# Gates projected a half block ahead, ranks and token transposes a step later: one reordering of a gated linear attention and mixture-of-experts kernel

## The chip, the cores and the metric

The kernel runs on one core of one Trainium2 chip. A core has TensorE (PE in the profile; its weight loads are PEld), VectorE (DVE), ScalarE (ACT), GpSimd (POOL) and SyncE (SP), which here only issues transfers. Each engine works through its own queue in order and waits on semaphores of the others. The metric is the device time of one execution in microseconds (us), the median of several runs.

## What is computed

The input x is 4 sequences of 2048 tokens with 256 features. The result is x plus two branches, both of the layer-normalised x:

```python
x = L0_attn_x
xn = _layernorm(x, axis=-1)
x = x + _L0_attn_ref(xn, ...) + _L0_ffn_ref(xn, ...)
```

The attention branch is a gated linear attention with 8 heads, keys of 128 and values of 64 features:

```python
q = (x @ Wq).reshape(B, S, H, DK)
k = (x @ Wk).reshape(B, S, H, DK) * DK ** (-0.5)
v = (x @ Wv).reshape(B, S, H, DV)
alpha = jax.nn.sigmoid((x @ Wg + bg) / GATE_NORM)
def step(state, inp):
    qt, kt, vt, at = inp
    state = at[..., None, None] * state + kt[..., None] * vt[:, :, None, :]
    return (state, jnp.einsum('bhk,bhkv->bhv', qt, state))
...
og = jax.nn.sigmoid(x @ Wog)
return out * og @ Wo
```

The other branch routes each token to 8 of 64 experts, which lie in 8 groups. The score of a group is the sum of its two best experts, the best 4 groups stay, and the 8 best experts within them are taken. An expert takes at most 256 tokens, in token order.

```python
group_scores = jax.lax.top_k(sfc.reshape(n, G, E // G), 2)[0].sum(-1)
gidx = jax.lax.top_k(group_scores, TG)[1]
...
topk_idx = jax.lax.top_k(tmp, K)[1]
pos = jnp.take_along_axis(jnp.cumsum(oh, 0) - 1, e[:, None], 1)[:, 0]
valid = pos < CAP
y = jnp.einsum('eci,eih->ech', jax.nn.silu(g) * u, w_down)
```

## The kernel before

**Two streams of work.** The attention goes through 32 blocks of 256 tokens (`block(s)`), each of two chunks (`ck`) of 128 tokens and two halves of 4 heads (`half`). A *unit* (s, half, ck) is one chunk of one half. The recurrence is done chunk by chunk: within a chunk by a masked product of scores, between chunks by a state of 128 x 64 per head. Beside it runs the routing, in batches of 512 tokens: `front(b)` normalises tokens, transposes them and makes the logits, `decays(i)` makes the decay factors of a group of batches, `back(b)` picks groups and experts and counts. All 16 batches are routed during the first 16 blocks. From block 16 on, the side stream is the experts.

**Steps.** `front`, `decays` and `back` are generators. `block` calls `step()` 12 times, and each call moves every generator that is due by one `yield`. Batch b's `back` starts at step 12 b + 3 (step 12 b + 1 is the first of block b), `front(b)` for b over 2 at step 12 (b - 2), and `decays` at a step set in the list near the end. When block 16 begins, the list of generators must be empty; then the memory of the routing is given to the experts.

**Order on the queues.** The order of the calls is a program order. A scheduler then makes each engine's queue from it by a model of time of its own, so that the order of a queue follows the program only roughly. `tc.issue_after(x)` keeps what is issued within it behind x.

**A half block**, on TensorE: state products of the two units done before (`dp`), decay differences (`lp`), keys of two groups of heads (`wk`), scores (`sp`), queries (`wq`), transposes of the keys (`kp`), the output projection of the chunk before (`wo`), values of the next block (`wv`), scores, gate (`wog`), and at the end the outputs (`od`) of two units. Each projection is three matmuls (high part by high part, high by low, low by high) in 16-bit parts. A projection of two heads or of one half of the gate is 12 matmuls of 128 x 256.

**The names that matter below.** In `project` the tile `pj` comes from the pool `ps["pj"]` with 4 buffers in this stage; a buffer is free when its readers are done. `split` (lines 220 and 221) reads it twice: ScalarE writes the high part (`k`, `qh`), then VectorE the low part (`k`, `ql`). VectorE also makes `qt` (line 860). `unit_a` makes the scores `sp` (one buffer), `unit_m` multiplies them on VectorE by the decay factors `dc` (line 929). `outputs` (lines 945 and 951) needs that product, the state and, on VectorE, the gate: `oT` is `od` times `og` plus 1 (line 959). `states` makes `dp` and, on VectorE, the new state (lines 979 and 982). `gate` makes one half of the heads' gate `og` with Tanh on ScalarE (line 827). `turn_tokens` transposes 512 tokens (`tp`, line 330) after ScalarE (line 390) and GpSimd (line 391) have made their two parts `x16`, and VectorE copies them out (line 331).

In `back`, lines 511 to 514 compare the group scores with one another: VectorE makes `cg` and `ce`, GpSimd masks and adds them. Then VectorE reduces `rank` (line 516), makes `gm` and `pen` (518, 520), GpSimd makes `tmp` (522, 523), VectorE takes maxima (530), replaces them (533) and makes `sel` (536). TensorE counts (`cp`, 541), VectorE makes `cr` (552), which SyncE stores to `cnt_d` (555). The first thing the experts do is read these counts back (line 594) and take differences on VectorE (`dd`, line 597).

**The start.** Before block 0, queries, keys, values and both gates of block 0 are made (`gate(0, 0)`, `gate(0, 1)`), then the first unit: scores, transposed keys, product and outputs. The units of which outputs and states are due stand in the list `done`.

Of the kernel before, what the change touches and what calls it, by code (L numbers as in the profile page):

```python
# [62 lines left out]
def bc(ap, axis, n):  # L63

    a = ap.unsqueeze(axis)
    shape = list(a.shape)
    shape[axis] = n
    return a.to_broadcast(shape)
# [3 lines left out]
def gla_moe_kernel(ctx: ExitStack, tc: tile.TileContext, x, Wq, Wk, Wv, Wo, Wg, bg, Wog,  # L72
# [70 lines left out]
    made = {}  # L143
# [180 lines left out]
    def turn_tokens(x16, xT):  # L324
        for t in range(0, RT, 2):
            tp = ps["mo"].tile([P, 2, 2, 2, P], F16, tag="mo", name="tp")
            for t2 in range(2):
                for a in range(2):
                    for c in range(2):
                        nc.tensor.transpose(tp[:, t2, a, c, :], x16[:, t + t2, a, c * P:(c + 1) * P], identh)  # L330
            nc.vector.tensor_copy(xT[:, t:t + 2], tp)

    def front(b):
# [61 lines left out]
                                       in_=flat.bitcast(F32)).ins  # L395
        yield True
        if b >= 2:
            turn_tokens(x16, xT)
            yield True
        stored = nc.sync.dma_start(out=xT_d[b], in_=xT)  # L400
# [78 lines left out]
    def back(b):  # L479
# [32 lines left out]
        nc.vector.tensor_tensor(ce, ga, gb, ALU.is_equal)  # L512
        nc.gpsimd.tensor_tensor(ce, ce, bc(tri, 1, RT), ALU.mult)
        nc.gpsimd.tensor_tensor(cg, cg, ce, ALU.add)
        rank = r1.tile([P, RT * G], F32, name="rank")
        nc.vector.tensor_reduce(rank, cg.rearrange("p t a b -> p (t a) b"), AX.X, ALU.add)
        gm = r1.tile([P, RT * G], F32, name="gm")
# [195 lines left out]
    def expert_late():  # L713

        for eng, lo, full, hi in moe["late"]:
            eng.tensor_tensor(lo, full, hi, ALU.subtract)  # L716
        moe["late"] = []

    def expert_step(new):

        q = list(moe["at"])
        if not new:

            q = [it for it in q if it[2] == len(expert_stages) - 1]
        if new and moe["next"] < E:
            e = moe["next"]
            moe["at"].append([e, fetch(e), 0])
            moe["next"] += 1
            look(e + AHEAD + 1)
        mids = []  # L730
        for it in q:
            e, m, st = it
            if st == len(expert_stages):
                continue
            expert_stages[st](e, m)
            if st == 2:
                mids.append((e, m))
            it[2] += 1
        for e, m in mids:
            expert_split(e, m)  # L740
        moe["at"] = [it for it in moe["at"] if it[2] < len(expert_stages)]


    side = []
# [4 lines left out]
    def step():  # L749

        now = clock[0]
        clock[0] += 1
        with ExitStack() as es:
            if len(anchor) > 1:
                es.enter_context(tc.issue_after(anchor[-2]))
            for it in list(side):
                if it[0] <= now and next(it[1], None) is None:
                    side.remove(it)
        if "at" in moe:
            owed[0] += EXPERTS / STEPS  # L760
            new = owed[0] >= 1.0
            if new:
                owed[0] -= 1.0
            expert_late()
            if new or moe["next"] >= E:
                expert_step(new)
# [52 lines left out]
    def two_heads(t, i):  # L819
        return t[:, :, 2 * i:2 * i + 2, :].rearrange("p c h t -> p c (h t)")  # L820

    def gate(s, i):

        if i == 0:
            blk[s]["og"] = ogp.tile([P, NCK, 4, P], F32, name="og")
        pj = project(s, "wog", i * 2 * P, P)
        nc.scalar.activation(two_heads(blk[s]["og"], i), pj, AF.Tanh, scale=og_fit)
# [66 lines left out]
    def unit_l(s, half, ck):  # L894

        B = blk[s]
        h0 = half * 4
        lp = ps["pj"].tile([P, 4, P], F32, tag="pj", name="lp")
        nc.tensor.matmul(lp.rearrange("p h i -> p (h i)"), lhsT=B["aj"][:, ck, :],  # L899
                         rhs=B["mv"][ck][:, h0:h0 + 4, :].rearrange("p h i -> p (h i)"),  # L900
                         start=True, stop=True)
        dc = dcp.tile([P, 4, P], F32, name="dc")
        nc.scalar.activation(dc, lp, AF.Relu, scale=-1.0)
        nc.scalar.activation(dc, dc, AF.Exp, scale=-1.0)

        if "at" in moe:
            nc.vector.tensor_tensor(dc, dc, bc(u_le, 1, 4), ALU.mult)
        else:
            nc.gpsimd.affine_select(out=dc, in_=dc, pattern=[[0, 4], [1, P]], compare_op=ALU.is_ge,
                                    fill=0.0, base=0, channel_multiplier=-1)  # L910
        B["dc", half, ck] = dc
# [14 lines left out]
    def unit_m(s, half, ck):  # L926
        B = blk[s]
        dc = B["dc", half, ck]
        anchor.append(nc.vector.tensor_tensor(dc, B["sp"], dc, ALU.mult).ins)  # L929
# [33 lines left out]
    def states(units):  # L963

        units = [u for u in units if (u[0] * NCK + u[2] + 1) % (SEQ // P)]
        if not units:
            return
        dp = ps["pj"].tile([P, 2, 4, DV], F32, tag="pj", name="dp")
        for n, (s, half, ck) in enumerate(units):
            kt, vw = blk[s]["kt"][half][:, ck * 8:ck * 8 + 8], blk[s]["vw"][ck]  # L970
            with tc.issue_after(made["od"]):
                for i in range(4):
                    product(dp[:, n, i, :], (kt[:, i, :], kt[:, 4 + i, :]),
                            tuple(t[:, half * 4 + i, :] for t in vw))
        for n, (s, half, ck) in enumerate(units):
            B = blk[s]
            new = w2.tile([P, 4, DV], F32, tag=f"state{half}", name=f"state{half}")
            if (s * NCK + ck) % (SEQ // P) == 0:
                nc.vector.tensor_copy(new, dp[:, n])
            else:  # L980
                B["aux"].tensor_tensor(new, state[half], bc(B["wall"][half][:, ck, :], 2, DV), ALU.mult)
                nc.vector.tensor_tensor(new, new, dp[:, n], ALU.add)
            state[half] = new
# [45 lines left out]
    done = []  # L1029

    def block(s):

        n = s + 1 < NS
        states(done)
        if s:
            split_o(s - 1, 1)
        if n:  # L1040
            load_block(s + 1)
            load_el(s + 1, 0)
        unit_l(s, 0, 1)
        keys(s, 1, 0)
        step()
        unit_a(s, 0, 1)
        keys(s, 1, 1)
        unit_l(s, 1, 0)
        step()
        unit_m(s, 0, 1)  # L1050
        queries(s, 1, 0)
        step()
        queries(s, 1, 1)
        turn_keys(s, 1, 0)
        if s:
            output(s - 1, 1)
        step()
        if s:
            finish(s - 1)
        if n:  # L1060
            values(s + 1, 0)
        unit_a(s, 1, 0)
        turn_keys(s, 1, 1)
        if s:
            gate(s, 1)
        step()
        unit_m(s, 1, 0)
        done[:] = (s, 0, 1), (s, 1, 0)
        outputs(done)
        step()  # L1070

        states(done)
        split_o(s, 0)
        if not n:
            unit_l(s, 1, 1)
            unit_a(s, 1, 1)
            output(s, 0)
            unit_m(s, 1, 1)
            outputs([(s, 1, 1)])
            split_o(s, 1)  # L1080
            step()
            return
        load_el(s + 1, 1)
        unit_l(s, 1, 1)
        keys(s + 1, 0, 0)
        step()
        unit_a(s, 1, 1)
        keys(s + 1, 0, 1)
        unit_l(s + 1, 0, 0)
        step()  # L1090
        unit_m(s, 1, 1)
        queries(s + 1, 0, 0)
        step()
        queries(s + 1, 0, 1)
        turn_keys(s + 1, 0, 0)
        output(s, 0)
        step()
        values(s + 1, 1)
        unit_a(s + 1, 0, 0)
        turn_keys(s + 1, 0, 1)  # L1100
        gate(s + 1, 0)
        step()
        unit_m(s + 1, 0, 0)
        done[:] = (s, 1, 1), (s + 1, 0, 0)
        outputs(done)
        step()
# [90 lines left out]
    def start_front(b):  # L1197
        return 0 if b < 2 else 6 if b == 2 else (b - 2) * STEPS

    for b in range(NB):  # L1200
        if b:
            f = front(b)
            side.append((start_front(b), f))
            if b == 1:
                with after(made["lt2"]):
                    next(f)
        side.append((b * STEPS + (3 if b else 0), back(b)))
        for i, (b0, nb_) in enumerate(DGROUPS):
            if i and b0 + nb_ - 1 == b:
                side.append((start_front(b) + (11 if b > 2 else 6), decays(i)))  # L1210

    unit_l(0, 0, 0)
    unit_a(0, 0, 0)
# [2 lines left out]
    step()  # L1216
    unit_m(0, 0, 0)
    done.append((0, 0, 0))
    outputs(done)
    for s in range(NS):  # L1220
        if not side and "at" not in moe:
            for _ in lists():
# [43 lines left out]
```

## Time and profile before

| | |
|---|---|
| median of 3 runs | 1251.77 us (1251.25 to 1252.61) |
| the profiled execution | 1252.01 us, its span 1250.0 us |
| blocks 2 to 15 (with routing), each | 34.3 us on the mean |
| blocks 17 to 29 (with experts), each | 41 to 44 us |
| TensorE's granted clock over the span | 0.995 of full |
| transfers over the span | 139 GB/s |

The span is the time from the first to the last instruction that the profile shows. The length of a block is the distance between the VectorE products of line 929, of which every block has four. In rows of the profile, a line gives start, duration, engine, source line, operation, what is written and read, and in brackets the idle time of the engine just before and what ended it. TensorE's matmuls overlap in the pipeline: one of 128 x 256 lasts 0.27 us in its row, and the next starts 0.11 us after it. So the distance from start to start, not the duration, is what a matmul costs when TensorE is full. Tables of stretches give the busy time of each engine in a stretch; the column after the five engines is the granted clock of TensorE.

### The profile page before, as it was taken

The numbers are of one execution on the slowest core, as the hardware profiler recorded it, in microseconds if no ns is written. First come the engines' busy times: TensorE is split into PE (matmuls) and PEld (weight loads), VectorE is DVE, ScalarE is ACT, GpSimd is POOL, SyncE is SP. The second block draws the span as 40 slices with busy tenths as digits, with TensorE's granted clock in tenths as the row PEclk, the third lists the DMA queues.
The fourth block names the chain that finished last, engine by engine and source line by source line (L and its number), as shares of the span: only waits on it lengthen the run. The fifth ranks groups of instructions, "written<-read, shape, count | busy, mean of one in ns | idle before, by whom it ended". The sixth has DMA issues, their size and how long they took to land.

```text
span 1250.0 us, 34808 instructions
## 1 busy us (share of the span) xinstructions
PE 1191.4 (95%) x13783; PEld 1040.7 (83%) x13783; DVE 973.5 (78%) x2669; ACT 857.5 (69%) x1536; POOL 709.3 (57%) x899
## 2 busy tenths in 40 slices
PE   6799999989999999999899999999999999999997
PEld 6587888877888878878789989999988898998986
DVE  6987778786787877777878878787878788887674
ACT  4567666666667567654667777777777777778764
POOL 1476667765666566653426656637757567565330
PEclk9899999999999999999999999999999999999999
DMA  7434444434334443323637676767767678666531
GB/s 244 158 123 127 131 122 117 126 87 114 97 112 127 135 127 110 108 52 78 181 87 152 163 160 137 169 151 178 157 156 167 148 167 180 150 138 150 111 60 35
DMA packets 148579, 165.35 MB, mean 132 GB/s; under 512 B 32384, under 2 KB 119296, under 8 KB 147712
## 3 DMA queue, kind: packets, MB, share of 16 engines
q1 hardware_dynamic: 114896, 113.57, 29.6%
q0 software_dynamic: 29712, 45.89, 21.5%
q10 hardware_dynamic: 3808, 3.67, 0.8%
q8 instruction: 108, 1.77, 0.6%
q14 instruction: 55, 0.45, 0.1%
HBM read 115.98 MB, written 58.38 MB: 139 GB/s over the span
## 4 chain that ended last, share of the span: by engine, by line
PE 68%; DVE 13%; POOL 6%; ACT 5%; DMA 5%; issue 3%; SPq 1%; DVEq 0%; POOLq 0%; ACTq 0%
PE pj L269 11%; PE pj L271 11%; PE pj L270 11%; PE od L945 4%; PE kp L884 3%; PE od L951 3%; DMA el<-el_d 3%; PE gu L269 2%; PE gu L271 2%; PE gu L270 2%; PE xet L646 2%; PE sp L270 2%; PE sp L269 2%; PE sp L271 2%; PE lp L899 1%
## 5 line engine op out<-in xcount | busy, mean ns | idle before, releaser
L702 POOL DMA_INDIRECT out_dram<-y,idx x128 | 211.6, 1653 | 93.1 <-issue 25.4
L626 POOL DMA_INDIRECT xe<-xw_d,idx x128 | 133.5, 1043 | 127.2 <-ACT y L688 86.9
L269 PE MATMUL pj<-xs,wq_h 128*128 128x256 f16 x496 | 135.4, 273 | 6.6 <-DVE k L221 4.6
L269 PE MATMUL pj<-xs,wk_h 128*128 128x256 f16 x496 | 135.6, 273 | 0.0
L271 PE MATMUL pj<-xs,wk_l 128*128 128x256 f16 x496 | 135.5, 273 | 0.0
L270 PE MATMUL pj<-xs,wk_h 128*128 128x256 f16 x496 | 135.5, 273 | 0.0
L270 PE MATMUL pj<-xs,wq_h 128*128 128x256 f16 x496 | 135.2, 273 | 0.0
L271 PE MATMUL pj<-xs,wq_l 128*128 128x256 f16 x496 | 135.2, 273 | 0.0
L929 DVE TENSOR_TENSOR dc<-sp,dc 128x512 f32<-128x512 f32 x128 | 87.7, 685 | 45.8 <-PE sp L271 28.4
L221 DVE SCALAR_TENSOR_TENSOR k<-pj,k 128x512 f16<-128x512 f32 x128 | 87.1, 683 | 40.1 <-ACT k L220 40.1
L220 ACT ACTIVATE k<-pj 128x512 f16<-128x512 f32 x128 | 75.2, 591 | 55.4 <-PE pj L271 55.1
L945 PE MATMUL od<-dc,v 128*64 128x128 f32 x1024 | 101.5, 280 | 7.3 <-DVE dc L929 7.3
L270 PE MATMUL sp<-ql,k 128*128 128x128 f16 x512 | 96.1, 220 | 5.5 <-DVE ql L221 5.2
L269 PE MATMUL sp<-qh,k 128*128 128x128 f16 x512 | 98.2, 220 | 0.0
L271 PE MATMUL sp<-qh,k 128*128 128x128 f16 x512 | 96.1, 220 | 0.0
L220 ACT ACTIVATE qh<-pj 128x512 f16<-128x512 f32 x128 | 76.0, 597 | 27.0 <-PE pj L271 26.8
L951 PE MATMUL od<-qt,state 128*64 128x128 f32 x960 | 94.4, 273 | 0.0
L989 ACT CAST oh<-oT 128x512 fp32r<-128x512 f32 x64 | 39.6, 618 | 79.5 <-DVE oT L959 79.5
L221 DVE SCALAR_TENSOR_TENSOR ql<-pj,qh 128x512 f16<-128x512 f32 x128 | 86.8, 679 | 9.2 <-ACT qh L220 9.1
L716 DVE TENSOR_TENSOR wl<-w,wh 128x768 fp32r<-128x768 f32 x64 | 61.2, 956 | 40.9 <-ACT wh L650 39.3
L884 PE MATMUL kp<-identh,k 128*128 128x128 f16 x1024 | 83.0, 220 | 8.7 <-DVE k L221 5.4
L860 DVE SCALAR_TENSOR_TENSOR qt<-pj,el 128x512 f32<-128x512 f32 x128 | 86.7, 678 | 0.0
(408 smaller groups left out, 4533.6 us busy)
## 6 DMA issues: line engine op xcount, KB each, us to landing
el<-el_d SPq DMA_DIRECT2D x64, 512.0 KB
xw_d<-x SPq DMA_DIRECT2D x16, 512.0 KB
xT_d<-xT SPq DMA_DIRECT2D x16, 512.0 KB
out_dram<-in_L_attn_x_dram SPq DMA_DIRECT2D x16, 512.0 KB
w<-in_L_ffn_w_gate_dram SPq DMA_DIRECT2D x64, 128.0 KB
w<-in_L_ffn_w_up_dram SPq DMA_DIRECT2D x64, 128.0 KB
w<-in_L_ffn_w_down_dram SPq DMA_DIRECT2D x64, 128.0 KB
xs<-xT_d SPq DMA_DIRECT2D x31, 256.0 KB
```

The costliest lines, as they stand in the source:

```text
L220: return (nc.scalar.activation(hi, t, AF.Copy, scale=scale).ins, nc.vector.scalar_tensor_tensor(lo, in0=t, scalar=scale, in1=hi, op0=ALU.m ...
L221: nc.vector.scalar_tensor_tensor(lo, in0=t, scalar=scale, in1=hi, op0=ALU.mult, op1=ALU.subtract).ins)
L269: nc.tensor.matmul(out_, lhsT=a[0], rhs=b[0], start=first, stop=False)
L270: nc.tensor.matmul(out_, lhsT=a[0], rhs=b[1], start=False, stop=False)
L271: return nc.tensor.matmul(out_, lhsT=a[1], rhs=b[0], start=False, stop=last).ins
L626: in_turn(lambda: nc.gpsimd.indirect_dma_start(out=xe[:, f, :], out_offset=None, in_=xw_d[:, :], in_offset=bass.IndirectOffsetOnAxis(ap=id ...
L702: two = [in_turn(lambda: nc.gpsimd.indirect_dma_start(out=of, out_offset=bass.IndirectOffsetOnAxis(ap=idx[:, e, f:f + 1], axis=0), in_=m[" ...
L860: read = nc.vector.scalar_tensor_tensor(qt, in0=pj, scalar=QFIT, in1=two_heads(el, i), op0=ALU.mult, op1=ALU.mult)
L884: nc.tensor.transpose(kp[:, i, :], k[:, i, :], identh)
L929: anchor.append(nc.vector.tensor_tensor(dc, B["sp"], dc, ALU.mult).ins)
L945: mm = nc.tensor.matmul(od[i * DV:(i + 1) * DV, n, j, :], lhsT=v[:, h0 + 2 * j + i, :], rhs=dc[:, 2 * j + i, :], start=True, stop=first)
L951: mm = nc.tensor.matmul(od[i * DV:(i + 1) * DV, n, j, :], lhsT=state[half][:, 2 * j + i, :], rhs=qt[:, ck, 2 * j + i, :], start=False, sto ...
```

## The change

Five edits in the order of calls; no computation is added or left out.

- The outputs of the first unit move from the end of the start into block 0, behind two more groups of keys.
- As no outputs have been made by then, the first `states` has nothing to stand behind, and does without.
- The gates of block s + 1 are made in the two halves of block s: the first half in the first, the second in the second. Before, the gate of the first half was made in the second half of block s, and that of the second half in the first half of block s + 1.
- `back` yields once more ahead of `rank`, so that `rank` and all behind it come a step later. It then ends in the twelfth step of its block and not in the eleventh.
- `front` of batches 3 and on yields once more ahead of `turn_tokens`, and `decays` of these starts a step later.

```diff
@@ front
         if b >= 2:
+            if b > 2:
+                yield True
             turn_tokens(x16, xT)
             yield True
@@ back
         nc.gpsimd.tensor_tensor(cg, cg, ce, ALU.add)
+        yield True
         rank = r1.tile([P, RT * G], F32, name="rank")
@@ states
-            with tc.issue_after(made["od"]):
+            with tc.issue_after(made["od"]) if "od" in made else ExitStack():
@@ block, first half
         keys(s, 1, 1)
         unit_l(s, 1, 0)
+        if s == 0:
+            outputs(done)
         step()
...
         turn_keys(s, 1, 1)
-        if s:
-            gate(s, 1)
+        if n:
+            gate(s + 1, 0)
         step()
@@ block, second half
         turn_keys(s + 1, 0, 1)
-        gate(s + 1, 0)
+        gate(s + 1, 1)
         step()
@@ the list of generators
-                side.append((start_front(b) + (11 if b > 2 else 6), decays(i)))
+                side.append((start_front(b) + (12 if b > 2 else 6), decays(i)))
@@ the start
     done.append((0, 0, 0))
-    outputs(done)
     for s in range(NS):
```

`n` is true in all blocks but the last.

## The prediction

> **What bounds the kernel now.** I read the page's first part, then the engines' busy time by stretch, then TensorE's waits, and last the single stalls in order of time.
>
> ```profile
> PE 1191.4 (95%) x13783; PEld 1040.7 (83%) x13783; DVE 973.5 (78%) x2669; ACT 857.5 (69%) x1536; POOL 709.3 (57%) x899
> ```
>
> TensorE is busy for 1191.4 of 1250.0 us, so 58.6 us of idle TensorE is all that reordering can win. The stretches show where it lies (columns: us, length, then busy time of PE, PEld, DVE, ACT and POOL with instruction counts, granted clock, DMA share, GB/s):
>
> ```profile
> 66.00:580.00 514.00, 488.68 (x5901) 414.44 (x5902) 404.50 (x1199) 336.79 (x606) 331.28 (x587) 1.00 0.38 111
> 580.00:650.00 70.00, 65.22 (x741) 55.77 (x739) 52.45 (x147) 42.81 (x75) 24.40 (x24) 1.00 0.51 132
> 650.00:1180.00 530.00, 528.67 (x6003) 477.13 (x6001) 422.81 (x1072) 403.81 (x730) 317.74 (x236) 1.00 0.69 156
> 1180.00:1250.00 70.00, 63.21 (x730) 54.65 (x728) 41.10 (x80) 38.07 (x66) 15.07 (x10) 0.99 0.27 50
> ```
>
> From 650 to 1180 us (attention with experts) TensorE idles 1.3 us: nothing to win. From 66 to 580 us (attention with routing, blocks 1 to 15) it idles 25.3 us, in the hand-over to the experts 4.8 us, in the last stretch 6.8 us, and the rest, 20 us, before 66 us. The waits by cause:
>
> ```profile
> PE od L945 <- DVE dc L929: 7.3, 5, 2.9
> PE kp L884 <- DVE k L221: 5.4, 4, 1.8
> PE sp L270 <- DVE ql L221: 5.2, 8, 1.7
> PE pj L269 <- DVE k L221: 4.6, 7, 0.9
> PE tp L330 <- ACT x L390: 4.6, 3, 2.2
> ```
>
> **The change part by part.** TensorE, VectorE, ScalarE, GpSimd and SyncE get the same instructions, each as often as before (22450 on TensorE with its weight loads, 39 activation-table loads on ScalarE among them). Only places in the queues move, so the sum is made of stalls.
>
> *(a) The first unit's outputs follow the keys.* Stalls of TensorE that bear on this and the next parts (start, length, what waits, idle time before it and its releaser):
>
> ```profile
> 50.05 1.12 PE L945 MATMUL od<-dc,v 128*64 128x128 f32 x8 [2.91 <-DVE dc L929]
> 65.91 0.88 PE L945 MATMUL od<-dc,v 128*64 128x128 f32 x12 [2.27 <-DVE dc L929]
> 231.27 0.29 PE L330 MATMUL tp<-identh,x 128*128 128x128 f16 x2 [2.14 <-ACT x L390]
> 373.52 0.22 PE L270 MATMUL sp<-ql,k 128*128 128x128 f16 x1 [0.62 <-DVE ql L221]
> 441.03 0.28 PE L330 MATMUL tp<-identh,x 128*128 128x128 f16 x2 [2.18 <-ACT x L390]
> ```
>
> At 47.14 us TensorE stands before the first outputs until VectorE has made dc. Now the state products and the keys go first, and the 2.91 us look won. They are not, because VectorE is full here: from 50 to 66 us its rows follow each other with hardly a gap. In the new order of VectorE the product dc of the third unit (65.18 us now) has before it the same work, plus one copy of transposed keys (0.33 us from its start to the next start): about 65.5 us. So TensorE, which waits for that product at 65.91 us, gets there no earlier, and the stall only spreads: the lower key halves (55.90 and 59.93 us now) come at about 58.1 and 58.8 us by adding up the rows ahead of them in the new order, and TensorE's queries wait for the first of them. What can be won is the clock:
>
> ```profile
> 49.00:50.00 1.00, 0.00 (x0) 0.00 (x0) 0.69 (x2) 0.00 (x0) 0.57 (x3) 1.00 0.02 6
> 51.00:52.00 1.00, 1.00 (x15) 0.77 (x14) 0.86 (x6) 0.00 (x0) 0.01 (x1) 0.50 0.00 0
> 68.00:69.00 1.00, 1.00 (x20) 0.93 (x18) 1.00 (x3) 0.00 (x0) 1.00 (x2) 0.50 0.00 0
> ```
>
> After each of the two idle stretches the granted clock is 0.5 for some 3.4 us (0.55, 0.50, 0.50, 0.75 from 50 to 54 us; 0.58, 0.50, 0.50, 0.71 from 67 to 71 us), a loss of 1.7 us each. The first lies under VectorE's bound; the second does not, since TensorE has no wait from 66 to 96 us. With the idle time spread over more places I give the second back half the time: **-0.9 us**. Ends: -8.6 (2.91 + 2.27 + 2 x 1.7), were VectorE not the bound; +1.6, were all that the lower key halves come later to reach the end.
> The Trainium skill (TensorE: Matmul & The Clock Gate, "HAM oscillation") states that only idle gaps over about 3.4 us cost the clock. By that rule gaps of 2.91 and 2.27 us cost nothing and this term is 0; the trace shows half clock after both, and full clock after the 2.14 us at 231 us, so the rows decide.
>
> *(b) Gates half a block ahead.* A gate group is 12 matmuls of 0.11 us, start to start: 1.3 us. Every half block keeps one; block 0's first half gains one, the last block's loses one. In block 0 it falls into the idle 63.6 to 65.9 us and is free. In the last block the gate runs from 1234.43 to 1235.73 us and the outputs start at 1235.95 us; their factor dc is there at 1234.88 us. Without the gate they start at about 1235.0 us, as dc then ends the wait: **-0.9 us**. The cover that is gone is thus counted. Its activation (0.69 us of ScalarE) moves along; VectorE's oT has no wait for og in the trace. Ends: -1.3, 0.
>
> *(c) Token transposes a step later* (blocks from batch 3 on, 13 batches). At 231 and 441 us they wait 2.14 and 2.18 us for ScalarE's casts, at 96.68 us 0.30 us: 4.6 us. A step is 34.3 us / 12 = 2.86 us (dc rows at 94.15 and 574.42 us lie 14 blocks apart), more than each wait, so the casts are done. With them go the store of xT, the copy of x to the output, the gate logits, the table load for the sigmoid and the decays, all a step later on SyncE and ScalarE; the tokens are read by projections blocks later, so nothing waits. I keep 1.0 us for a new wait of the same size as the smaller ones in the list (0.2 to 0.9 us): **-3.6 us**. Ends: -4.6, +1.
>
> *(d) Ranks a step later.* In a half block of today (VectorE rows of one place):
>
> ```profile
> 371.02 0.61 DVE L530 MAX8 m<-tmp 128x8 f32<-128x64 f32 x4 [0.46 <-POOL tmp L523]
> 372.44 0.43 DVE L536 TENSOR_TENSOR sel<-tmp,rep 128x256 bf16<-128x256 f32 x1
> 372.78 0.68 DVE L221 SCALAR_TENSOR_TENSOR ql<-pj,qh 128x512 f16<-128x512 f32 x1
> 373.38 0.68 DVE L860 SCALAR_TENSOR_TENSOR qt<-pj,el 128x512 f32<-128x512 f32 x1
> ```
>
> ScalarE has qh at 372.17 us, yet ql starts at 372.78 us, behind the maxima, replacements and sel; TensorE's sp waits 0.62 us. In the new order keys, ql and qt mostly stand ahead of maxima and sel, and keys ahead of rank. In blocks 1 to 15 the waits for ql are 2.5 us in all (0.62, 0.18, 0.62, 0.62, 0.50) and for qt 0.9 us. I take 70% of 3.4: **-2.4 us**. The waits of projections for k (0.5 to 0.9 us each) I leave: there k waits for ScalarE behind a 1.28 us table load, and rank, gm and pen ahead of it run meanwhile. Ends: -7.0 (those 3.6 us and a further 1.0 too), +5 (second rival, its smaller form).
>
> *(e) Hand-over to the experts.* The counts of the last batch are also a step late: VectorE's cr stands just ahead of oT (585.36 us now) and not at 581.30 us, so some 3.5 us later, and the store (4.64 us) and reload (2.42 us) of the counts follow it. VectorE's first dd waits 3.25 us for them now and would wait about 4.2 us, the second 1.3 instead of 2.64 us, since keys and state now go ahead of the first. **0**. Ends: -1.5, and +2.9, the whole step.
>
> Sum: -0.9 - 0.9 - 3.6 - 2.4 + 0 = -7.8 us; the span goes from 1250.0 to 1242.2 us. The profiled execution took 1252.01 us, 2.0 us around its span, and the median is 1251.77: 0.24 less. So 1242.2 + 2.0 - 0.2 = **1244 us**.
>
> **The rivals.**
> *The whole VectorE side clears.* All waits for ql, qt and k at kp (3.6 us) go, 2.1 us of dc waits, the tp waits and most of the start: 4.6 + 3.4 + 3.6 + 2.1 + 0.9 + 6.9 = 21.5, or 1230 us. For it: VectorE is only 78% busy. Against: k is late behind ScalarE.
> *Ranks overfill a quarter (slower).* Between the products of the units (s,1,1) and (s+1,0,0) VectorE now has rank 0.42, gm and pen 1.27, maxima and replacements 1.28, sel 0.33, two xT 1.2, k 0.6, two ql and qt 2.4, kt 0.33, dc 0.6: 8.4 of the 8.6 us of a quarter block. Waits inside (0.3 for k, 0.6 for sp, 0.5 for POOL's cg) make an overrun of 1.2 us. TensorE's cover from sp to od is a gate and eight transposes, 1.3 + 0.44, of which dc takes 0.69: 1.06 us. Cost per batch is the overrun above that. At 1.2 us it takes 13 x 0.14 = 2 us; from 1.64 us on it eats the 7.8; at 2.2 us (gm at its longest, 0.92, and one more wait of POOL) it costs 14.8 and gives 1259 us. Against: sel, cr and xT may slip past dc in the queue, and in part do.
> *Only gate and tp pay*, as ql finds other work ahead of it: -4.5, and 1247.3 us.
> *The waits only move* and the change does nothing: 1251.8 us. For it: ScalarE's table loads and its wait for oT (2.96 us at 192 us) stay where they were.
>
> **How the numbers follow.** Forecast 0.42 (its own range 1239 to 1248), all of VectorE's side 0.15, gate and tp only 0.20, nothing 0.08, overfilled quarter 0.15. A measurement of this kernel tells about 0.2%, 2.5 us, from no change. Faster: 0.42 + 0.15 + 0.20 = 0.77; same 0.08; slower 0.15. The range, 1232 to 1255 us, leaves out some six tenths of each outer case (0.09 + 0.09, under 2 in 10).
>
> **What would show it.** (a) No 2.91 us stall at 47 us, dc of the third unit still near 65 us, granted clock near 1.00 from 67 to 71 us. (b) Outputs of the last block within 0.3 us of dc. (c) No tp wait over 1 us. (d) sp waits for ql under 1.5 us from 66 us on. (e) TensorE idle 4 to 6 us from 580 to 650 us. Wrong if TensorE idles as long as now from 66 to 580 us, or od waits for dc in most blocks.

## The result and the profile after

The changed kernel takes 1248.22 us (median of 10 runs, 1245.44 to 1249.80), the kernel before beside it 1252.45 us (10 runs, 1251.25 to 1254.33). The ratio is 0.9955, 95% interval 0.9943 to 0.9967: faster by 0.45%, which would be 5.6 us; the two medians lie 4.2 us (0.34%) apart, which the interval holds too. The profiled execution took 1247.5 us, its span 1245.6 us against 1250.0, so 4.4 us are to be found in the traces.

The engines' totals in the profile after: the counts of instructions are the old ones and TensorE is as busy as before, so the gain is idle time.

```profile
PE 1191.6 (96%) x13783; PEld 1039.2 (83%) x13783; DVE 967.7 (78%) x2669; ACT 858.6 (69%) x1536; POOL 710.5 (57%) x899
```

The stretches of the profile after (columns as in the prediction's table):

```profile
66.00:580.00 514.00, 490.73 (x5900) 415.45 (x5899) 397.12 (x1194) 336.75 (x605) 331.35 (x585) 0.99 0.38 112
580.00:650.00 70.00, 67.21 (x767) 58.14 (x764) 56.40 (x161) 45.65 (x78) 24.90 (x25) 1.00 0.52 140
```

TensorE's idle time from 66 to 580 us, where most of the gain was expected, went from 25.3 to 23.3 us only. From 580 to 650 us, where none was expected, it went from 4.8 to 2.8 us. Fixed windows cut the kernels at different places of the work, so the rest of this document measures stages by the VectorE products `dc` (line 929 before, 932 after; the new lines shift the later ones by up to 3). Each stage is the distance between the same two products in both kernels; in us, after less before:

| stage | after - before |
|---|---|
| first instruction to the first product (49.31 us before) | -0.5 |
| first product to the end of block 0 | +1.8 |
| end of block 0 to block 14 | -3.3 |
| block 14 to block 15 | +1.5 |
| hand-over: block 15 to block 16 | -2.9 |
| block 16 to block 30 | 0.0 |
| last block, to the last instruction | -1.0 |

They add up to the 4.4 us. Up to the end of block 15 the net is -0.4 us. A single stage ahead of block 17 is less sure than its sum: with every mark taken one product later, the stages from the first product on read -0.1, +0.8, -3.8 and +0.3 in place of +1.8, -3.3, +1.5 and -2.9. From block 17 to block 30 the distance to the old trace is the same to 0.1 us: TensorE is full there, and what was won ahead of it is carried to the end unchanged.

TensorE's waits by cause (us, times, longest), here from 66 to 580 us alone and not over the whole span as in the prediction, after:

```profile
PE pj L269 <- DVE k L221: 7.2, 8, 1.3
PE od L948 <- DVE dc L932: 6.3, 5, 2.5
PE tp L330 <- ACT x L390: 1.9, 2, 1.6
```

Against the same window before, the two waits that the change was costed on did fall: `tp` from 4.6 to 1.9 us, `sp` for `ql` from 2.5 to 1.5 us; `kp` for `k` from 3.6 to 0.9 us. But the projections' wait for `k` rose from 3.6 to 7.2 us and that of the outputs for `dc` from 4.4 to 6.3 us.

**Where the 2.1 us of `tp` went.** ScalarE's rows around 228 us in the kernel before (start, length, line, operation; in brackets its idle time and what ended it):

```profile
225.21 0.62 ACT L989 CAST oh<-oT 128x512 fp32r<-128x512 f32 x1 [2.99 <-DVE oT L959]
...
230.61 0.60 ACT L390 CAST x<-xt 128x512 f16<-128x512 f32 x1
```

The same place after:

```profile
228.68 0.62 ACT L992 CAST oh<-oT 128x512 fp32r<-128x512 f32 x1 [2.62 <-DVE oT L962]
...
231.65 1.07 ACT L220 ACTIVATE k<-pj 128x512 f16<-128x512 f32 x2
```

and the stall of TensorE that belongs to it:

```profile
233.00 0.27 PE L269 MATMUL pj<-xs,wq_h 128*128 128x256 f16 x1 [1.11 <-DVE k L221]
```

In both kernels ScalarE stands nearly 3 us before a cast that waits for `oT`; behind it stand decay factors with a table load of 1.28 us (226.34 and 229.82 us) and, before, four pieces of the normalised tokens (2.06 us). Before, TensorE came to the transposes first and waited there (2.14 us at 231.27 us). Now the transposes are not yet due, and at the same point of its queue, behind the same 12 matmuls of a query projection, TensorE meets the next product of the same late ScalarE: the keys' split, without which no buffer for a projection is free. A stall of 2.14 us became one of 1.11 us. Over the stretch, ScalarE's waits for `oT` are 58.0 us before and 53.5 us after; the source of the lateness stayed.

**A quarter block that ranks overfill.** VectorE after, ahead of a stall of TensorE of 1.47 us at 277.83 us (`od` for `dc`):

```profile
275.75 0.85 DVE L462 TENSOR_TENSOR rs<-rs,lt 128x256 f32<-128x256 f32 x1
...
277.10 0.68 DVE L932 TENSOR_TENSOR dc<-sp,dc 128x512 f32<-128x512 f32 x1
```

From 269.24 us to here VectorE's rows follow each other without a gap: rank, penalties, queries, the decay factors' sums (`lt`, `rs`), maxima and replacements, and the product last. The same order gives 1.47 us once more at 414.70 us, and 0.66 us at 551.69 us. It is the second rival of the prediction in its smaller form, but only where a group of decay factors falls into the same quarter.

**The hand-over.** VectorE before, where the last counts are stored, read back and differenced (`dd`):

```profile
589.76 0.42 DVE L597 TENSOR_TENSOR dd<-c,c 64x512 f16<-64x512 f16 x1 [3.25 <-DMA c<-cnt_d]
590.10 0.40 DVE L982 TENSOR_TENSOR state<-state,dp 128x256 f32<-128x256 f32 x1
590.43 0.68 DVE L221 SCALAR_TENSOR_TENSOR k<-pj,k 128x512 f16<-128x512 f32 x1
...
594.35 0.42 DVE L597 TENSOR_TENSOR dd<-c,c 64x512 f16<-64x512 f16 x1 [2.64 <-DMA c<-cnt_d]
```

and after:

```profile
583.83 0.73 DVE L555 TENSOR_SCALAR cr<-cp,seen 64x512 f16<-64x512 f32 x1
...
585.84 0.41 DVE L985 TENSOR_TENSOR state<-state,dp 128x256 f32<-128x256 f32 x1
587.98 0.69 DVE L221 SCALAR_TENSOR_TENSOR k<-pj,k 128x512 f16<-128x512 f32 x1 [1.73 <-ACT k L220]
590.27 0.42 DVE L600 TENSOR_TENSOR dd<-c,c 64x512 f16<-64x512 f16 x1 [1.61 <-DMA c<-cnt_d]
...
594.33 0.42 DVE L600 TENSOR_TENSOR dd<-c,c 64x512 f16<-64x512 f16 x1 [0.59 <-DMA c<-cnt_d]
```

Before, the first `dd` waits 3.25 us for the reload and the state and the keys stand behind it, the second 2.64 us with keys (594.69 us) behind it. TensorE paid for that with 1.06 and 1.75 us, 2.8 us in all:

```profile
590.56 0.27 PE L269 MATMUL pj<-xs,wq_h 128*128 128x256 f16 x1 [1.06 <-DVE state L982]
595.42 0.29 PE L884 MATMUL kp<-identh,k 128*128 128x128 f16 x2 [1.75 <-DVE k L221]
```

After, the counts `cr` come 2.5 us later (583.83 against 581.30 us), the scheduler sets the state and the first keys ahead of the first `dd`, and the waits of VectorE shrink to 1.61 and 0.59 us. TensorE's largest stall of this stage is now 1.12 us.

### The profile page after: what moved, and what is told of

It reads as the page before. It is cut to its first block, busy times and chain, and to the rows that moved or that the text cites. A ratio compares the mean times of both kernels' runs of the same rounds, so it can differ in the third digit from the quotient of the medians.

```text
span 1245.6 us, 34787 instructions
## 1 busy us (share of the span) xinstructions
PE 1191.6 (96%) x13783; PEld 1039.2 (83%) x13783; DVE 967.7 (78%) x2669; ACT 858.6 (69%) x1536; POOL 710.5 (57%) x899
## 4 chain that ended last, share of the span: by engine, by line
PE 67%; DVE 14%; ACT 8%; DMA 4%; POOL 4%; issue 2%; SPq 1%; DVEq 0%; ACTq 0%; POOLq 0%
PE pj L269 11%; PE pj L271 11%; PE pj L270 11%; PE od L948 4%; PE od L954 3%; PE kp L887 3%; DMA el<-el_d 3%; PE gu L269 2%; PE gu L271 2%; PE gu L270 2%; PE xet L649 2%; PE sp L269 2%; PE sp L270 2%; PE sp L271 2%; DVE qt L863 2%
## 5 line engine op out<-in xcount | busy, mean ns | idle before, releaser
L906 ACT ACTIVATE dc<-lp 128x512 f32<-128x512 f32 x128 | 76.2, 596 | 13.2 <-PE lp L902 13.2
```

## The experiments

Ratios are to the kernel before on the same chip, with 95% intervals. The stage columns are us against the trace of before, from one profile each; the time up to the first product is left out. Stages with the same order of work repeat to within about 2 us up to block 15 and to 0.1 us from block 16 to 30. Each profile is one execution: that of only_ranks was the slowest of 12 (2.9 us above its median), those of only_gates and end_only lie 2.3 and 2.4 us below theirs. So the columns show places, and the ratios show what a kernel gains or loses. The columns also hold stretches of some 3.4 us in which TensorE's granted clock is 0.50, worth up to 1.7 us each. In the column to block 14 the trace of before has none, nor have only_outputs and end_only; the change, late_parts, no_outputs and no_ranks have one, only_gates, only_ranks and only_turns two; in the hand-over only_outputs, only_gates and no_ranks have one. The kernels of the second group ran on a chip on which the kernel before took 1282.11 us; their four traces show 19 to 22 us more from block 16 to block 30 than the trace of before. Of these only stages up to block 15 are comparable, and ratios within the group.

| kernel | median us | ratio | block 0 | to 14 | to 15 | hand-over | last |
|---|---|---|---|---|---|---|---|
| the change | 1248.22 | 0.9955 (0.9943 to 0.9967) | +1.8 | -3.3 | +1.5 | -2.9 | -1.0 |
| only_outputs | 1257.10 | 1.0026 (1.0015 to 1.0037) | +2.5 | +0.1 | +0.1 | +0.3 | 0 |
| only_gates | 1256.29 | 1.0019 (1.0009 to 1.0030) | 0.0 | +3.4 | -0.2 | +0.3 | -1.0 |
| only_ranks | 1256.78 | 1.0018 (1.0006 to 1.0031) | +1.3 | +9.4 | 0.0 | -2.8 | 0 |
| only_turns | 1253.54 | 0.9994 (0.9982 to 1.0005) | 0.0 | +1.7 | +1.1 | +0.2 | 0 |
| end_only | 1249.80 | 0.9967 (0.9956 to 0.9979) | 0.0 | -1.0 | +1.5 | -3.3 | -1.0 |
| late_parts | 1248.19 | 0.9955 (0.9938 to 0.9973) | -0.1 | +0.4 | +1.2 | -3.0 | -1.0 |
| no_outputs | 1247.11 | 0.9948 (0.9932 to 0.9965) | -0.3 | +0.2 | +0.4 | -3.2 | -1.0 |
| no_ranks | 1252.58 | 0.9996 (0.9982 to 1.0010) | +2.5 | -0.7 | -0.4 | +0.6 | -1.0 |

The expectations stand as they were written ahead of the runs. Two theories were set against each other: that the gain is made at the hand-over and in the last block alone (ranks of the last batch, gates of the last block), and that in blocks 1 to 15 the edits win what the prediction said but something takes it back (among the candidates: the table loads of ScalarE).

**One part of the change at a time.** The outputs alone, which are the edits at `states`, in block 0 and at the start:

```diff
         unit_l(s, 1, 0)
+        if s == 0:
+            outputs(done)
```

> The kernel before with the first part alone: the first unit's outputs behind two more groups of keys. Theory H (the gain sits at the hand-over to the experts, about 3.6 us, and comes with the last batch's ranks; 1 us more at the end comes with the gates; the rest only moves waits): no change, within 1 us of before, and the product of the third unit near 65 us. The prediction's sum: 0.9 us faster. A third theory, that the parts work only together: slower by 1 us or more.

Measured 1.0026, slower by 0.26% with block 0 at +2.5 us. The 2.91 us stall at 47 us is gone, but this order costs more than it saves.

The gates alone:

```diff
-        if s:
-            gate(s, 1)
+        if n:
+            gate(s + 1, 0)
...
-        gate(s + 1, 0)
+        gate(s + 1, 1)
```

> The kernel before with the gates half a block ahead and nothing else. Theory H: 1 us faster, all of it in the last block, nothing at the hand-over from 566 to 602 us. The prediction's sum: 0.9 us faster. If the gates are what helps at the hand-over (the gate's ScalarE work sat ahead of oT there): 4 to 5 us faster. Only together: slower.

Measured 1.0019. The last block gains its 1.0 us, blocks 1 to 14 lose 3.4, of which up to 3.4 us can be the two stretches at half clock (from 165.6 and 510.4 us) behind waits of 2.53 and 2.22 us: gates of equal number, half a block earlier, are not free there.

The ranks alone:

```diff
         nc.gpsimd.tensor_tensor(cg, cg, ce, ALU.add)
+        yield True
```

> The kernel before with the ranks a step later and nothing else. Theory H: 3 to 4 us faster, of which all at the hand-over (the distance between the last VectorE product of block 14's line and that of block 15's, 566 to 602 us, shrinks from 35.8 to about 32 us), and the stretch from 66 to 566 us as long as before. The prediction's sum: 2.4 us faster, spread over blocks 1 to 15, and the hand-over unchanged. Only together: slower.

Measured 1.0018. The whole gain at the hand-over is there (-2.8 us), and 9.4 us are lost ahead of it in this slowest of the 12 runs; by the medians, 3.4 us slower in all, some 6 us are lost. Its waits of TensorE from 66 to 580 us show where (the first of the list):

```profile
PE tp L330 <- ACT x L390: 7.8, 5, 2.5
```

With ranks a step later and the transposes in their old step, the transposes wait for their casts at five places instead of three, 7.8 us instead of 4.6.

The token transposes and decay factors alone:

```diff
         if b >= 2:
+            if b > 2:
+                yield True
             turn_tokens(x16, xT)
...
-                side.append((start_front(b) + (11 if b > 2 else 6), decays(i)))
+                side.append((start_front(b) + (12 if b > 2 else 6), decays(i)))
```

> The kernel before with the token transposes, and the decays with them, a step later and nothing else. Theory H: no change within 1 us, the waits of the transposes for ScalarE under 2.5 us in all but the waits of projections for keys up by as much. The prediction's sum: 3.6 us faster, spread over the batches. Only together: slower.

Measured 0.9994, no difference that can be told. Its first wait of TensorE from 66 to 580 us:

```profile
PE pj L269 <- DVE k L221: 10.3, 10, 2.5
```

No wait of `tp` for ScalarE's casts is left in its list, yet the projections' waits for `k` went from 3.6 to 10.3 us. What the place at 231 us showed holds over the stretch: the wait changes its name.

**The change less its transposes** (the second group):

> The changed kernel without its last part: token transposes and decays at their old step, the other parts as changed. If the later transposes are what makes up for the 10.4 us that ranks alone lost in blocks 1 to 14: those blocks lose 6 to 11 us against before and the whole is 2 to 7 us slower than before. If gates or outputs make up for it: as fast as the changed kernel within 2 us.

Measured 1.0040 (1.0013 to 1.0067) at 1287.11 us. Its product of block 14 lies about 10 us behind that of before, that of the whole change 2.0 us ahead. TensorE's waits in it:

```profile
PE tp L330 <- ACT x L390: 9.2, 5, 2.5
```

So the later transposes are worth some 9 us (by the medians, of two chips) to 12 us (by the traces) beside the later ranks, and nothing without them: the `tp` waits that the ranks bring (9.2 us here, 1.9 us in the change) are more than half of it. The two edits together stand about where the kernel before stood.

**Are table loads the holder?** Since the change leaves ScalarE's 39 table loads of 1.28 us where they were, they could be what takes the gain back. Twenty of them were taken out, in the changed kernel and in the one before:

```diff
-            nc.scalar.activation(sg[:, b], zs[:, b], AF.Sigmoid)
-            nc.scalar.activation(sc, lg[:, :, 0:E], AF.Sigmoid, scale=unfit[:, GATE:GATE + 1])
+            nc.scalar.activation(sc, lg[:, :, 0:E], AF.Tanh, scale=gate_fit)
...
+    nc.scalar.activation(sm, z, AF.Sigmoid)
```

> The changed kernel with 19 table loads on ScalarE in place of 39: the expert scores by a hyperbolic tangent, which needs no load beside the exponential, as twice the sigmoid less one, with twice the bias and the weights made from score plus one; and the sigmoid of the decay gates once for each group of batches. Two more small operations on GpSimd for each batch. Theory T (what is left of TensorE's waits in blocks 1 to 15 hangs on a load of 1.28 us ahead of the exponential and the keys): the waits of projections for keys and for ScalarE's dc fall from about 10 to under 4 us, and it is 4 to 9 us faster than the changed kernel. Rival S: no waits fewer in all, within 2 us of the changed kernel.

> The kernel before with the same 19 table loads in place of 39. Theory T: waits for keys and dc fall here too, 3 to 8 us faster than before; the waits of the transposes for ScalarE's casts shrink with them. Rival S: within 2 us of before.

Measured 0.9964 (0.9940 to 0.9988) and 1.0026 (1.0003 to 1.0048). The product of block 14 comes 2.6 and 6.3 us later than before, and TensorE is idle for 25.6 and 31.1 us from 66 to 580 us (23.3 and 25.3 with all table loads), though ScalarE's busy time there fell from 336.75 to 309.65 and from 336.79 to 307.95 us. Half the table loads gone won nothing, in kernels that also have two more small operations on GpSimd for each batch and queues in a new order. In the changed kernel the projections' wait for `k` fell from 7.2 to 1.1 us, that of the scores for `ql` rose to 4.9, and the outputs still wait 4.7 us for `dc`. The theory of the table loads, that the time comes back with them, falls.

**The ranks of the last batch alone** (also in the second group):

```diff
+        if b == NB - 1:
+            yield True
         rank = r1.tile([P, RT * G], F32, name="rank")
```

> The kernel before, with the ranks a step later in the last batch alone. Theory H (ranks pay only where the last batch hands over to the experts): the hand-over shrinks by 2.9 us as it did with ranks in all batches, and nothing else moves before block 15: 2 to 4 us faster than before. Rival S (each queue is made anew by the scheduler, and what it makes of the hand-over hangs on the stage before it): the hand-over between -1 and +3 us, no faster than before.

Measured 0.9997 (0.9972 to 1.0021), inconclusive: up to block 15 it stands as before (-0.1, -0.5, +0.2), its first two `dd` wait 2.11 us and not at all, but its hand-over has new waits of up to 5.2 us on that chip and its stage is 9.5 us longer. Between the first and the third product of block 16 all four kernels of that chip lose 5 to 12 us against the trace of before. Up to the first of these products, counted from the first of block 15, ranks_last is 2.4 us shorter than before, and tables_before, with the old ranks, is 0.3 us longer; but one product later, behind a stretch at half clock from 598.5 us on, only 0.4 us are left. Hence the next kernel, on another chip.

**Only the end of the change.** Ranks later in the last batch, gates ahead from block 14 on, everything else as before:

```diff
+        if b == NB - 1:
+            yield True
         rank = r1.tile([P, RT * G], F32, name="rank")
...
-        if s:
+        if 0 < s <= 14:
             gate(s, 1)
+        if n and s >= 14:
+            gate(s + 1, 0)
...
-        gate(s + 1, 0)
+        gate(s + 1, int(s >= 14))
```

> The kernel before, with the ranks a step later in the last batch alone and the gates half a block ahead from block 14 on; outputs, transposes and all other batches as before. Its queues stand as in the kernel before up to block 14 and as in the changed kernel from the hand-over on. Theory H (the whole gain is the hand-over and the last block): 3.5 to 4.5 us faster than before, as fast as the changed kernel; hand-over 2.9 us shorter, last block 1 us shorter. Rival (the gain needs the routing stage of the changed kernel): 0 to 1.5 us faster.

Measured 0.9967 (0.9956 to 0.9979), which overlaps the interval of the whole change. Compared row by row, TensorE's order is that of the kernel before up to 551 us and that of the changed kernel from 561 us to the end. VectorE's first two differences in it:

```profile
590.47 0.42 DVE L599 TENSOR_TENSOR dd<-c,c 64x512 f16<-64x512 f16 x1 [1.67 <-DMA c<-cnt_d]
...
594.44 0.42 DVE L599 TENSOR_TENSOR dd<-c,c 64x512 f16<-64x512 f16 x1 [0.51 <-DMA c<-cnt_d]
```

The waits are those of the changed kernel (1.61 and 0.59 us), and so are the stages: -3.3 at the hand-over behind +1.5 in block 15, -1.0 in the last block. The products of block 13 and the first three of block 14 stand at -1.0 us and those from block 17 to 30 at -3.5, so the hand-over is worth 2.5 us net. One batch's ranks and the gates of the last blocks bring the gain; the outputs, the transposes and 15 of 16 batches' ranks are not needed for it.

**The change less its ranks**, the counter-test:

> The changed kernel with the ranks at their old step; outputs, gates and transposes as changed. Theory H: it lacks the gain of 2.9 us at the hand-over from block 15 to 16 and keeps the 1 us of the last block; blocks 1 to 14 lie within 4 us of the changed kernel; the whole 0 to 4 us slower than before. Rival (ranks do nothing for the hand-over): the hand-over as short as in the changed kernel.

Measured 0.9996 (0.9982 to 1.0010): no gain. The last block still gains 1.0 us, the hand-over nothing (+0.6, with a stretch at half clock from 597.3 us on behind a wait of 2.48 us), and the two differences together wait as long as before (5.7 against 5.9 us):

```profile
589.36 0.47 DVE L599 TENSOR_TENSOR dd<-c,c 64x512 f16<-64x512 f16 x1 [2.36 <-DMA c<-cnt_d]
...
594.73 0.42 DVE L599 TENSOR_TENSOR dd<-c,c 64x512 f16<-64x512 f16 x1 [3.37 <-DMA c<-cnt_d]
```

**The change less its outputs**, as the outputs alone cost 0.26%:

> The changed kernel with the first unit's outputs back at their old place. If that part costs in the changed kernel what it costs alone (3 us, all in block 0): 2 to 3 us faster than the changed kernel. The prediction's term: 0.9 us slower than it. If the parts work only together: slower by 3 us or more.

Measured 0.9948 (0.9932 to 0.9965). Block 0 is at -0.3 us against +1.8 in the change, as expected, but by block 16 the two stand equal, counted from the first product. Its interval covers that of the change; whether the outputs cost anything beside the other parts is not told apart.

**A version from the best stretches.** Each part was to start where its trace began to win: ranks and gates from block and batch 5 on, transposes and decay factors from batch 6 on, outputs unchanged.

```diff
+            if b >= 6:
+                yield True
             turn_tokens(x16, xT)
...
+        if b >= 5:
+            yield True
...
-        gate(s + 1, 0)
+        gate(s + 1, int(s >= 5))
```

> The kernel before, with ranks later from batch 5, transposes and decays from batch 6 and gates ahead from block 5 on. Up to block 4, where the changed kernel lost 3.6 us, it stands as before, and from block 7 on as the changed kernel, which from there gained 8 us on the kernel before. If stretches of the queue add up: 7 to 8 us faster than before, 3 us faster than the changed kernel. If the seam costs it: 2 to 5 us faster than before.

Measured 0.9955 (0.9938 to 0.9973), the same as the change. The queues came out as planned: row by row, the order of all four engines is that of the kernel before up to 201 us and that of the changed kernel from 319 us on. What was to be won was lost between the two, at the seam: at the end of block 4 this kernel is 3.7 us ahead of the change (-0.1 against +3.6 us to the trace of before), at the end of block 7 only 0.4 us (+1.5 against +1.9). In the seam TensorE waits 2.49 us for the casts of the transposes at 230.36 us and runs at half clock behind it. No version was found that beats the changed kernel by more than the intervals.

## Why the prediction was right, and where its steps were wrong

The sign and the range held: -7.8 us were predicted on the span, -4.4 us came, and 1248 us lies 4 us above the forecast. That the range held is in part luck, as the mechanism was half wrong: the gain was made at two places, the last block (b), as said, and the hand-over (e), which stood in the sum at zero, while the 6.0 us of (c) and (d) did not come.

**(a) outputs, -0.9.** The mechanism was read rightly. The third unit's `dc` is at 65.03 us (about 65.5 said), the lower key halves are at 56.91 and 57.60 us (about 58.1 and 58.8 said), and of the 2.91 us stalls of 1.30 and 0.87 us are left in block 0. The gain did not come: up to the end of block 0 the change stands at +1.4 us (-0.6 one product later), and the edit alone at +2.5 in block 0 and 0.26% slower in all. The clock part was half right: TensorE still waits for the third unit,

```profile
65.77 1.55 PE L948 MATMUL od<-dc,v 128*64 128x128 f32 x12 [2.53 <-DVE dc L932]
```

and the mean granted clock is 0.66 from 65 to 70 us. It is 1.00 from 45 to 60 us, where before it fell to a mean of 0.66 from 50 to 55 us. So the first stretch at half clock went, and the second, which I had given back half, stayed. Another came from 99.4 us on, where the trace of before has none, so that the change has as many of them as before.

**(b) gates, -0.9.** Right at the place: the last block is 1.0 us shorter in every kernel of the table that has the edit and in none without it. The last outputs of the first half start at 1231.59 us, 0.23 us after TensorE began to wait, and within 0.1 us of the end of `dc` (1230.85 + 0.69). What I left out is that the edit alone costs in blocks 1 to 14 (3.4 us in its trace, two stretches at half clock among them), where I let the moved gates be free.

**(c) transposes, -3.6, and (d) ranks, -2.4.** Both waits fell, but by less than was said: `tp` by 2.7 of its 4.6 us and `ql` by 1.0 of its 2.5. At one place the casts were not done a step later: the transposes that waited 0.30 us at 96.68 us now wait 1.59 us at 99.40 us. The failed step is that I booked a removed wait as time won: "more than each wait, so the casts are done" prices the stall and not what TensorE meets when it runs on. In blocks 1 to 15 the change stands at -1.8 us; end_only, whose transposes and ranks up to the last batch are the old ones, stands at +0.5, and no_outputs, which has both edits, at +0.5 too: nothing that can be told from zero is left of -6.0. The one stretch at half clock that the change and no_outputs have there can hide up to 1.7 us of a gain, no more. Shown for it are the stall that became one of 1.11 us at `k`, the 1.47 us at `dc` twice, and the kernels with one of the two edits, in which the waits only change their names. Also missed: ranks and transposes hold each other up. Ranks alone cost some 6 us by the medians (9.4 us in the trace), and with the later transposes these are gone. Through which of ScalarE's instructions the later ranks make the casts late was not followed, and stays open.

**(e) hand-over, 0.** This is the other term that failed, -2.9 us by its stage and 2.5 us net in end_only. I had the new order right ("keys and state now go ahead of the first") and then priced only the waiting instruction: 4.2 us for the first `dd`, 1.3 for the second, where 1.61 and 0.59 us were measured. Two steps were mis-sized. The chain from counts to reload does not take the fixed 4.64 + 2.42 us: the reload was issued 4.7 us after the store before and 2.2 us after it now (582.06 to 586.75, and 585.05 to 587.27 us), so the counts came back nearly as early though they were made 2.5 us later. Before, SyncE issued a load of `xs` 1.2 us behind the store, and the DMA engines were busy 92% of the time from 582 to 586 us; now no such load stands there, and from 585 to 587 us they were busy 46%. Whether that is why the store took longer was not tested. And the two stalls of TensorE behind those waits, 2.8 us, which are in the trace of before, were not put into the sum. That the later ranks are the cause is shown by three kernels: without them the gain is gone (no_ranks), without the moved gates it is there (only_ranks), and with the last batch's ranks and the gates from block 14 on alone it is there as well (end_only). Whether the last batch's ranks bring all of it without any moved gate is not shown, as ranks_last was inconclusive.

Three of the marks failed: TensorE idles 2.8 us and not 4 to 6 us from 580 to 650 us, a `tp` wait of 1.59 us is over 1 us, and the granted clock from 67 to 71 us is 0.79 and not near 1.00. The count of 22450 TensorE instructions is in no view; the profile has 13783 matmuls and as many weight loads in both kernels.

Of the rivals, "the waits only move" describes blocks 1 to 15, and the overfilled quarter occurs at two places for 1.47 us each and at a third for 0.66 us, not at every batch. "Only gate and tp pay" would have come nearest in time (1247.3 us), for a wrong reason.

## What to carry to other kernels

A stall that a reordering removes is won only up to the next thing that waits for the same late engine: ask what that is before booking it, and afterwards compare stages between the same two instructions, not waits by name. Where one stage hands over to the next through memory, look at what stands behind the waiting instruction in its engine's queue; here 2.5 to 2.9 us lay in one such place, and moving a single batch's work by a step, beside the gates of the last blocks, won them. Under a scheduler the parts of a change don't add up (alone they gave +0.26%, +0.19%, +0.18% and -0.06%, together -0.45%), so test them alone, together, and each one left out.

## What the runs showed of the hardware

- The length of a stall did not by itself decide whether the granted clock was halved behind it. In the change, stalls of 1.30 and 0.87 us in block 0 left it at 1.00 and one of 2.53 us halved it, but in only_outputs one of 2.52 us (until 235.49 us) left it at 1.00. At 99.40 us a stall of 1.59 us halved it in the change; in no_turns, with the same order of work up to there, one of 1.58 us did not. The Trainium skill (TensorE: Matmul & The Clock Gate, "HAM oscillation") puts the limit at idle gaps of about 3.4 us; these traces disagree once more, with half clock behind 2.53 and 1.59 us. What decides it was not looked for. The row and the stretch at 99 us in the change, then in no_turns (the granted clock is the third number from the end of a stretch):

```profile
99.40 0.40 PE L330 MATMUL tp<-identh,x 128*128 128x128 f16 x2 [1.59 <-ACT x L390]
99.00:102.00 3.00, 2.60 (x8) 1.11 (x9) 2.19 (x4) 2.11 (x5) 2.84 (x3) 0.57 0.00 0
...
99.43 0.29 PE L330 MATMUL tp<-identh,x 128*128 128x128 f16 x2 [1.58 <-ACT x L390]
99.00:102.00 3.00, 2.57 (x29) 1.86 (x30) 2.20 (x4) 2.65 (x6) 2.84 (x3) 1.00 0.00 0
```

- With 20 of 39 table loads of 1.28 us taken from ScalarE, TensorE's idle time in the routing stage did not fall (23.3 to 25.6 us). ScalarE is busy for 66% of that stretch (336.75 of 514 us) and yet late for TensorE; having less to do did not make it early here. That the order of its queue is what makes it late is argued, not shown.
- On one chip every kernel was some 2% slower, the one before at 1282.11 us, with the loss behind block 15 in the four kernels that were traced; up to there ranks_last, whose order is the old one, agreed with the trace of before to 0.5 us by stage. The cause was not looked for.
